# The first pair's expert layers as 64-row half products, and value sums and router additions on GpSimd

## The chip, the cores and the metric

The kernel runs on one core of a Trainium2 chip. The metric is the device time of one execution in microseconds (us). Five engines matter: TensorE (PE in the profile), VectorE (DVE), ScalarE (ACT), GpSimd (POOL) and the queue of SyncE (SP), which only issues DMAs here. Each engine takes its instructions in the order in which the program gives them.

## What is computed

There are 8 samples of 512 tokens and 256 features, each with 64 context rows and one conditioning row. In short:

```python
nx = layer_norm(x)                                  # (8, 512, 256)
weights = softmax(nx @ Wq @ (context @ Wk).T / 16)  # over 64 context rows
evidence = weights @ (context @ Wv)
combined = concat([nx, evidence, cond])             # 768 features
router_probs = softmax(combined @ router_W + router_b)          # 3 experts
h = silu(combined @ e_w1[e] + e_b1[e])              # 512 per expert
routed = sum over e of router_probs[e] * (h @ e_w2[e] + e_b2[e])
g = sigmoid(silu(combined @ gate_w1 + gate_b1) @ gate_w2 + gate_b2)
out = x + g * (routed @ out_w + out_b)
```

All of it is float32. A float32 product of 512 columns appears in the trace as two matmul instructions.

## The kernel before

Samples are worked in four pairs, j = 0 to 3. The two samples of a pair are the columns of a 2 x 2 block product, so that the nx part of each pair of hidden chunks takes seven products (called P1 to P7 here, `nx_operands`) in place of eight, over the sums T of the samples (`combine_x`) and ws of the weights (`combine_weights`, on GpSimd). The hidden layer has 14 chunks of 128: two of the gate (group 0) and twelve of the experts (groups 1 to 6). An expert layer e = 0, 1, 2 works two groups, `PAIRS[e]`, called a and b.

A group has three PSUM banks: U takes P1, P6, P7 and P4 in turn and is read after P1 (`keep_part` 0,0), after P6 (1,0), after P7 (`add` 1,1) and at the end (`silu` 0,1). Y takes P2 and is read by `add` 0,0. Z takes P5, is read by `keep_part` 1,1, then takes P3 and is read at the end. `keep_part` is a ScalarE copy to SBUF, `add` a VectorE addition to what is there, `silu` a ScalarE activation. The evidence part of every chunk is a product over only 64 context rows of each sample (`evidence`): sample 0 on rows 0 to 63 of the array and sample 1 on rows 64 to 127, the two side by side, in a stretch of its own between the layers.

In pairs 1 to 3 (`half_layers`) the nx products are also cut into a product over rows 0 to 63 and one over rows 64 to 127. A table of slots names two half products for each slot, which run side by side. The halves of one product lie two slots or more apart, and `half_product` makes TensorE wait for one half's end before the other half adds to the same bank. In pair 0 (`expert_layer`) the nx products are full, 128 rows. Between them stand, at points named S, A, B, C, D and E, the steps that `put(within, (e, point), ...)` places there: the second layer's weights e_w2 @ out_w (`second_layer`, eight products of 256 columns for each expert), the value products of pair 1 (`values_together`, products c1, c3, c5, c6 with sums of weights and values made by GpSimd and by accumulating DMAs), value weights of expert 2 (`value_weights`), the router of pair 0, the statistics and normalisation of pair 1's x, and the spread of the router's probabilities (`spread_probabilities`: four small DMAs to DRAM, then one that broadcasts them to all partitions, tile pb). `weigh` multiplies finished hidden chunks by them. `late_rows`, between layers 0 and 1, holds products with 32 columns of the array in bank 2, which VectorE reads.

The order in every engine's queue is the order of the program text (`tc.manual_schedule(engines=None)`). Waits between engines are placed by the framework.

## Time and profile before

| | us |
|---|---|
| median of 3 runs (lowest to highest) | 450.2 (450.2 to 450.43) |
| the profiled execution, its own time | 450.17 |
| its span, first to last instruction | 448.0 |
| TensorE busy | 443.1 (99%) |
| VectorE busy | 364.8 (81%) |
| ScalarE busy | 229.3 (51%) |
| GpSimd busy | 170.7 (38%) |

The profile shows one execution. Times on its axis begin at the span's start. The first pair's expert layers lie between 33.7 and 101.5 us, with the granted clock at 1.0 throughout. A busy TensorE is one with an instruction in flight; how close its instructions follow each other is read from their starts.

### The profile page before, as it was taken

How to read it: one execution, taken by the hardware profiler on the slowest of the kernel's cores; microseconds unless marked ns; L12 is line 12 of the kernel's file. 1: busy time of each engine (PE TensorE's matmuls, PEld its weight loads, DVE VectorE, ACT ScalarE, POOL GpSimd, SP SyncE). 2: the span in 40 equal slices, each digit the busy share in tenths (PEclk: the TensorE clock that was granted, in tenths of full speed). 3: DMA queues.
4: the chain of work that ended last, by engine and by line, in shares of the span. 5: the costliest groups of instructions: out<-in, count | busy, mean ns of one | idle time of the engine just before them, and what ended most of it. 6: DMA issues, size and time to landing. Idle time of an engine off the chain costs nothing.

```text
span 448.0 us, 5750 instructions
## 1 busy us (share of the span) xinstructions
PE 443.1 (99%) x1807; PEld 233.2 (52%) x1807; DVE 364.8 (81%) x686; ACT 229.3 (51%) x417; POOL 170.7 (38%) x219
## 2 busy tenths in 40 slices
PE   9999999999999999999999999999999999999996
PEld 8744646444444444444666444445666444445665
DVE  3888889677978999879886989879867846689875
ACT  3545685548424257678523187668251266766000
POOL 6566777530241157108738320000466500001360
PEclk9999999999999999999999999999999999999999
DMA  8987798655651579979974284710561392000715
GB/s 254 381 192 177 112 260 166 116 93 117 64 85 23 119 172 234 166 131 115 121 119 69 36 216 127 112 30 11 83 95 28 53 217 41 1 0 5 112 25 94
DMA packets 136182, 51.20 MB, mean 114 GB/s; under 512 B 107069, under 2 KB 129529, under 8 KB 135641
## 3 DMA queue, kind: packets, MB, share of 16 engines
q1 hardware_dynamic: 113776, 29.90, 32.0%
q0 software_dynamic: 15456, 19.90, 24.8%
q10 hardware_dynamic: 6921, 1.05, 1.4%
q8 instruction: 14, 0.23, 0.2%
q14 instruction: 15, 0.12, 0.1%
HBM read 31.23 MB, written 7.39 MB: 86 GB/s over the span
## 4 chain that ended last, share of the span: by engine, by line
PE 98%; DMA 1%; SPq 0%; DVE 0%; issue 0%; DVEq 0%
PE ps_u L1139 32%; PE ps_z L1139 13%; PE ps_y L1139 12%; PE ps_X L1139 7%; PE ps_Y L1139 7%; PE ps_V L1139 3%; PE ps_gu L1139 3%; PE ps_vc L1139 3%; PE ps_Z L1139 3%; PE ps_w2o L556 2%; PE ps_W L1139 2%; PE ps_vw L930 2%; PE ps_s L795 2%; PE ps_gz L1139 2%; DMA hall<-in_ctx_dram 1%; PE ps_tokens L1139 1%
## 5 line engine op out<-in xcount | busy, mean ns | idle before, releaser
L1139 PE MATMUL ps_u<-nxT,w 64*128 64x512 f32 (+1 forms) x184 | 86.8, 592 | 0.0
L1254 DVE TENSOR_TENSOR hall<-hall,pb 128x512 f32<-128x512 f32 x96 | 62.9, 694 | 12.2 <-ACT hall L1197 11.8
L1197 ACT ACTIVATE hall<-hall,abias 128x512 f32<-128x512 f32 x72 | 49.4, 718 | 25.0 <-DVE hall L1203 24.7
L1139 PEld LDWEIGHTS ps_u<-nxT,w 64*128 64x128 f32 (+1 forms) x184 | 33.1, 187 | 26.1 <-issue 21.8
L1139 PE MATMUL ps_z<-T,ws 64*128 64x512 f32 (+1 forms) x92 | 46.4, 590 | 0.0
L1139 PE MATMUL ps_z<-nxT,ws 64*128 64x512 f32 (+1 forms) x92 | 45.9, 590 | 0.0
L1139 PE MATMUL ps_y<-nxT,w 64*128 64x512 f32 (+1 forms) x92 | 45.5, 590 | 0.0
L1139 PE MATMUL ps_u<-T,ws 64*128 64x512 f32 (+1 forms) x92 | 42.8, 590 | 0.0
L1139 PE MATMUL ps_u<-T,w 64*128 64x512 f32 (+1 forms) x98 | 42.4, 589 | 0.0
L1206 ACT COPY hall<-ps_u 128x512 f32<-128x512 f32 x48 | 27.8, 579 | 13.2 <-PE ps_u L1139 12.5
L1634 POOL TENSOR_TENSOR hall<-hall 128x1026 f32<-128x1026 f32 x5 | 14.0, 2790 | 50.1 <-DVE hall L1631 50.1
L1139 PE MATMUL ps_z<-wT,vw 64*128 64x512 f32 x56 | 27.5, 596 | 0.0
L1631 DVE TENSOR_TENSOR hall<-hall 128x1026 f32<-128x1026 f32 x21 | 26.3, 1267 | 0.4
L1139 PEld LDWEIGHTS ps_z<-nxT,ws 64*128 64x128 f32 (+1 forms) x92 | 17.3, 188 | 13.3 <-issue 10.9
L1139 PE MATMUL ps_z<-wT,w 64*128 64x512 f32 x48 | 24.1, 589 | 0.0
L1139 PEld LDWEIGHTS ps_y<-nxT,w 64*128 64x128 f32 (+1 forms) x92 | 17.3, 188 | 13.0 <-issue 12.8
L1139 PEld LDWEIGHTS ps_z<-T,ws 64*128 64x128 f32 (+1 forms) x92 | 17.2, 188 | 12.8 <-issue 11.1
L1139 PEld LDWEIGHTS ps_u<-T,w 64*128 64x128 f32 (+1 forms) x98 | 16.2, 187 | 13.2 <-issue 12.1
L1139 PEld LDWEIGHTS ps_u<-T,ws 64*128 64x128 f32 (+1 forms) x92 | 16.1, 188 | 13.3 <-issue 11.7
L1203 DVE TENSOR_TENSOR hall<-hall,ps_z 128x512 f32<-128x512 f32 x24 | 16.3, 683 | 6.3 <-ACT hall L1206 3.0
L1197 ACT ACTIVATE hall<-ps_u,abias 128x512 f32<-128x512 f32 x24 | 16.4, 686 | 8.9 <-PE ps_u L1139 4.5
L594 POOL DMA_DIRECT2D other<-hall x1 | 1.3, 1332 | 50.1 <-ACT other L1664 50.1
(375 smaller groups left out, 1096.1 us busy)
## 6 DMA issues: line engine op xcount, KB each, us to landing
pb<-pd POOLq DMA_DIRECT2D x4, 1536.0 KB, 7.0
xb<-in_x_dram SPq DMA_DIRECT2D x64, 64.0 KB, 2.5
x<-in_x_dram SPq DMA_DIRECT2D x28, 128.0 KB, 3.6
hall<-hall POOLq DMA_DIRECT2D x6, 513.0 KB, 5.8
w<-in_L_xcond_e_w_dram SPq DMA_DIRECT2D x6, 512.0 KB, 11.0
xd<-x SPq DMA_DIRECT2D x24, 128.0 KB, 3.5
xg<-xd SPq DMA_DIRECT2D x48, 64.0 KB, 2.7
hall<-in_L_xcond_e_w_dram SPq DMA_DIRECT2D x3, 512.0 KB, 15.5
```

Of the source, the lines that this page charges most:

```text
L556: nc.tensor.matmul(ps[:, d * H : (d + 1) * H], w2T[:, k, (i + d) * P : (i + d + 1) * P], ow_sb[:, k, :], start=(k == 0 and d == 0), stop=T ...
L594: nc.gpsimd.dma_start(dst, src, accum_op=ALU.add)
L795: nc.tensor.matmul(ps[side(i, h), g * NH : (g + 1) * NH], mr[:, k, 2 * j + i, g * TB : (g + 1) * TB], S["nxT", 2 * j + i][:, k, h * NH : ( ...
L930: nc.tensor.matmul(ps, vT[:, k, j * 2 * CT : (j + 1) * 2 * CT], w1[:, KH + k, n0:n1], start=(k == 0), stop=(k == KH - 1),)
L1139: return nc.tensor.matmul(ps, lhsT, rhs, start=start, stop=True, skip_group_check=not start)
L1197: nc.scalar.activation(h, h if src is None else src, AF.Silu, bias=abias[:, c, 2 * j + i : 2 * j + i + 1])
L1203: nc.vector.tensor_tensor(h, h, part, ALU.add)
L1206: nc.scalar.copy(chunk(n, i, d), part)
L1254: nc.vector.tensor_tensor(h, h, S["pb", j][:, i, :, 2 * q // RC, :], ALU.mult)
L1631: engine.tensor_tensor(at[dst], at[p], at[m], ALU.subtract)
L1634: engine.tensor_tensor(at[dst], at[p], at[m], ALU.add)
```

## The change

`expert_layer` gives way to `first_pair_layer`, which works by a table of slots as pairs 1 to 3 do. A slot names the product of the first 64 rows and that of the last 64, and then the steps that follow: kID.n is `keep_part` of sample I and chunk D for group n, aID.n is `add`, sID.n is `silu`, @X runs what is put at point X, wN weighs N chunks, mGI copies finished second-layer weights. Second-layer products (20.0 to 22.3, two products of 256 columns each), the value products c1, c3.0, c3.1, c5, c6 and the value weights of expert 2 (v.0, v.1) are half products in these slots too; the last c3 product moves into the gate of the outputs.

```diff
-    def expert_layer(j, e, steps):
-        a, b = PAIRS[e]
...
+    FIRST_PAIR = (
+        (
+            "P1.b P5.a |",
+            "P2.a P1.a |",
+            "P4.g P1.b | k00.b",
+            "P1.a P2.a | k00.a a00.a",
+            "P2.b P4.g |",
+            "P5.a P6.b | k11.a @A",
+            "P6.a P5.b |",
+            "P6.b P2.b | k10.b",
+            "P3.a P6.a | k10.a gate s00.a",
+            "P7.b v.1 |",
+            "P5.b v.0 | k11.b",
+            "P7.a P7.b | a11.b early @C",
+            "v.1 P3.a |",
+            "v.0 P7.a | a11.a a00.b @B v s00.b s11.a s11.b rest",
+            "P3.b P4.b |",
+            "20.3 20.0 |",
+            "P4.b P4.a |",
+            "20.2 20.1 |",
+            "P4.a P3.b |",
+            "20.0 20.3 |",
+            "20.1 20.2 | m00 m02 @D",
+        ),
+        (
+            "P2.a P1.a |",
+            "c6 P1.b |",
+            "P1.a P5.a | k00.a",
+            "P1.b P2.a | k00.b odd a00.a",
+            "P5.a c6 | k11.a @c6 @N @A",
+            "c1.0 P6.a |",
...
+            "P7.a c5 | a11.a",
+            "P3.a P7.b | a11.b early w10 s11.a s11.b rest",
...
+        (
+            "P1.b P1.a |",
+            "P2.a P5.a |",
+            "P1.a P1.b | k00.a k00.b odd w2",
+            "P2.b P2.a | a00.a",
+            "P5.a P6.a | k11.a w2",
+            "P6.b P2.b | a00.b w1 @W @A",
+            "P6.a P5.b | k10.a s00.a",
+            "P3.a P6.b | k10.b",
+            "c3.0 P7.a |",
+            "P5.b P7.b | k11.b s00.b",
+            "P7.a c3.0 | @c3.0 a11.a",
+            "P7.b P3.a | a11.b early @C w6 s11.a s11.b rest",
+            "P3.b P4.a |",
+            "c3.1 P4.b |",
+            "P4.a P3.b |",
+            "P4.b c3.1 | @c3.1 @D",
+        ),
+    )
...
+        def half(token, k):
+            if token not in units:
+                units[token] = unit(token)
+            rows = row_half(k)
+            for ps, lhsT, rhs, part in units[token]:
...
+                yield half_product(ps, lhsT[rows, :], rhs[rows, :], k, fresh_, part)
...
+        for slot in FIRST_PAIR[e]:
+            products, after = slot.split("|")
+            both = [half(token, k) for k, token in enumerate(products.split())]
+            while both:
+                both = [one for one in both if next(one, both) is not both]
+            for token in after.split():
+                step(token)
```

`evidence` uses `half_product` as well. The router's additions go to GpSimd, the maximum between them stays on VectorE, and the value sums go from the start of layer 1 to layer 0's point B:

```diff
-        nc.vector.tensor_tensor(lg[:, 1:, :], le, lg[:, 1:, :], ALU.add)
+        if close and ED - 1 in es:
+            logit_sums(j, nc.vector)
...
+    def logit_sums(j, engine, biased=False):
+        lg, le = S["lg", j], S["le", j]
+        if not biased:
+            logit_bias(j, engine)
+        engine.tensor_tensor(lg[:, 1:, :], le, lg[:, 1:, :], ALU.add)
         mx = work.tile([P, NJ], F32, tag="rmx", name=f"rmx_{j}")
         nc.vector.tensor_reduce(mx, lg.rearrange("p e j -> p j e"), AX.X, ALU.max)
-        nc.vector.tensor_tensor(
+        engine.tensor_tensor(
             lg, lg, mx.unsqueeze(1).to_broadcast([P, E, NJ]), ALU.subtract
         )
...
+        elif at == (0, "C"):
+            home("yb", "na4", "na2", "a5", "a3")
...
+            add(V["a5"], v(1, 1), v(2, 1))
+            sub(V["na4"], v(2, 1), v(3, 1))
...
                 put(within, (0, "B"), combine_weights, 1)
                 put(within, (0, "B"), combine_weights, 2)
+                put(within, (0, "B"), logit_sums, 0, nc.gpsimd, True)
+                put(within, (0, "B"), values_together, 0, "C")
                 put(within, (0, "B"), combine_gate)
+                put(within, (0, "D"), combine_second, 0)
-                put(within, (0, "A"), router_logits, 0)
+                put(within, (0, "A"), router_logits, 0, range(ED), False)
+                put(within, (0, "A"), logit_bias, 0, nc.gpsimd)
...
-                put(within, (0, "C"), router_exp, 0)
-                put(within, (0, "D"), router, 0)
...
-                put(within, (0, "D"), spread_probabilities, 0)
...
+                put(within, (1, "S"), transpose_second, 1)
+                put(within, (1, "S"), router_exp, 0)
+                put(within, (1, "S"), anchor_columns, 1)
...
+                    for b, point in ((b0, "S"), (b1, "N")):
+                        put(within, (1, point), normalize, b)
+                        put(within, (1, point), store_x, b)
+                    put(within, (1, "N"), router, 0)
+                    put(within, (1, "N"), spread_probabilities, 0)
-                    put(within, (1, "B"), router_part, b0)
+                    put(within, (1, "A"), router_part, b0)
...
-                put(within, (2, "A"), gate_differences, 0)
+                put(within, (2, "A"), gate_differences, 0, (0, 1))
+                put(within, (2, "C"), gate_differences, 0, (2, 3))
```

## Rows read from the trace of the kernel before

**Rows 1.** The page, part 1: busy us (share of the span) xinstructions of each engine.
```profile
PE 443.1 (99%) x1807; PEld 233.2 (52%) x1807; DVE 364.8 (81%) x686; ACT 229.3 (51%) x417; POOL 170.7 (38%) x219
```
**Rows 2.** Waits of TensorE over the span: total us, times, longest.
```profile
PE ps_wake L332 <- PEq L2203: 0.8, 1, 0.8
PE pt_ctx L349 <- DMA hall<-in_ctx_dram: 0.3, 1, 0.3
```
**Rows 3.** Timeline of TensorE, evidence 0 and layer 0: start, us, operation, count.
```profile
29.17 1.02 PE L1139 MATMUL ps_u<-nxT,w 128*128 128x512 f32 x2
30.12 0.69 PE L1139 MATMUL ps_y<-wT,vw 64*128 64x512 f32 x1
...
33.23 0.59 PE L1139 MATMUL ps_z<-wT,vw 64*128 64x512 f32 x1
33.75 1.98 PE L1139 MATMUL ps_u<-nxT,w 128*128 128x512 f32 x4
35.57 1.02 PE L1139 MATMUL ps_u<-T,w 128*128 128x512 f32 x2
...
48.45 3.62 PE L556 MATMUL ps_w2o<-ow_sb,hall 128*128 128x256 f32 x16
...
53.23 0.69 PE L1139 MATMUL ps_u<-wT,vw 64*128 64x512 f32 x1
```
**Rows 4.** Timeline of TensorE, pair 1's layers, first and last step.
```profile
158.02 0.59 PE L1139 MATMUL ps_y<-nxT,w 64*128 64x512 f32 x1
...
205.66 0.59 PE L1139 MATMUL ps_z<-nxT,ws 64*128 64x512 f32 x1
```
**Rows 5.** Timeline of VectorE in layer 0.
```profile
33.01 0.69 DVE L1203 TENSOR_TENSOR hg<-hg,ps_w 128x512 f32<-128x512 f32 x1 [0.45 <-PE ps_w L1139]
33.61 0.69 DVE L786 TENSOR_TENSOR T<-nxT,T 128x512 f32<-128x512 f32 x1
...
45.73 1.29 DVE L548 STREAM_TRANSPOSE hall<-hall 128x512 f32<-128x512 f32 x2
```
**Rows 6.** Timeline of ScalarE in layers 0 and 1.
```profile
34.91 0.58 ACT L1206 COPY hall<-ps_u 128x512 f32<-128x512 f32 x1 [2.19 <-PE ps_u L1139]
...
36.63 0.69 ACT L1197 ACTIVATE hg<-ps_u,abias 128x512 f32<-128x512 f32 x1 [0.27 <-PE ps_u L1139]
37.22 1.32 ACT L1197 ACTIVATE hg<-hg,abias 128x512 f32<-128x512 f32 x2
...
56.46 1.28 ACT L695 ACT_TABLE_LOAD   x1
57.75 0.49 ACT L695 ACTIVATE sd<-mv,eps_t 128x4 f32<-128x4 f32 x2
```
**Rows 7.** Timeline of GpSimd in layer 0 and after it.
```profile
43.35 0.63 POOL L267 TENSOR_TENSOR ws<-w 128x256 f32<-128x256 f32 x1
...
48.30 0.64 POOL L270 TENSOR_TENSOR ws<-w,ws 128x256 f32<-128x256 f32 x1
...
50.65 2.10 POOL L910 DMA_DIRECT2D pd<-prT  x4
55.06 0.56 POOL L914 DMA_DIRECT2D pb<-pd  x1 [2.31 <-DMA pd<-prT]
```
**Rows 8.** Timeline of VectorE, layers 0 and 1.
```profile
48.62 0.75 DVE L686 BATCH_NORM_STATS2 st<-x 128x6 f32<-128x256 f32 x2
...
53.37 0.52 DVE L500 STREAM_TRANSPOSE ar<-ps_late 128x128 f32<-128x128 f32 x2 [0.65 <-PE ps_late L657]
...
58.30 3.68 DVE L705 TENSOR_SCALAR x<-x,mv,rstd 128x256 f32<-128x256 f32 x4
...
62.10 1.88 DVE L705 TENSOR_SCALAR x<-x,mv,rstd 128x256 f32<-128x256 f32 x4
...
72.89 3.09 DVE L1254 TENSOR_TENSOR hall<-hall,pb 128x512 f32<-128x512 f32 x5
```
**Rows 9.** The page, part 6, DMA issues: KB each, us from issue to landing.
```profile
pb<-pd POOLq DMA_DIRECT2D x4, 1536.0 KB, 7.0
```

More of the change, by code (lines that the diff above doesn't have):

```diff
@@ L548, in transpose_second, with second_unit, keep_second @@
             nc.vector.transpose(w2["T"][:, k, :], w2[e][:, k, :])
[L550 to L561 removed]
+    def second_unit(ps, i, d):
+        return [
+            (ps, w2["T"][:, k, (i + d) * P : (i + d + 1) * P], ow_sb[:, k, :], ps[:, d * H : (d + 1) * H])
+            for k in range(KH)
+        ]
+    def keep_second(e, i, ps):
+        c = e * RC + i
+        nc.scalar.copy(w2o[:, c : c + 2, :].rearrange("p c n -> p (c n)"), ps)
     def combine_second(e):
@@ L1139, in product, with half_product @@
         return nc.tensor.matmul(ps, lhsT, rhs, start=start, stop=True, skip_group_check=not start)
-    def half_product(ps, lhsT, rhs, half, start=False):
+    def half_product(ps, lhsT, rhs, half, start=False, out=None):
         prior_half, prior = last_half.get(ps.name, (half, None))
         if prior_half == half or start:
-            ins = product(ps, lhsT, rhs, start)
+            ins = product(ps if out is None else out, lhsT, rhs, start)
         else:
@@ L1158, in half_product @@
             nc.tensor.wait_ge(*finished[tag])
-            ins = product(ps, lhsT, rhs, start)
+            ins = product(ps if out is None else out, lhsT, rhs, start)
             tc.declare_fence(ins.ins, group=group)
@@ L1185, in evidence @@
             half = slice(i * CT, (i + 1) * CT)
-            product(ps, values(j, c)[half, c * P : (c + 1) * P], S["wT", j][half, :], start=start)
+            half_product(
+                ps, values(j, c)[half, c * P : (c + 1) * P], S["wT", j][half, :], i, start=start
+            )
     def chunk(n, i, d):
@@ L1319, in run, with first_pair_layer @@
+    VALUE_STEPS = {(1, c) for c in ("c6", "c1.0", "c1.1", "c5", "c1.2", "c1.3")} | {(2, "c3.0"), (2, "c3.1")}
+    W2O_BANKS = {(0, 0): 0, (0, 2): 4, (1, 0): 7, (1, 2): 4, (2, 0): 7, (2, 2): 6}
+    def first_pair_layer(e, steps):
+        j = 0
+        ns = dict(zip("ab", PAIRS[e]), g=0)
+        units, opened = {}, set()
         def run(point):
@@ new lines, in half @@
+        def half(token, k):
[3 more added lines that the diff above has]
+            for ps, lhsT, rhs, part in units[token]:
+                fresh_ = ps.name not in opened and (
+                    token[:2] in ("P1", "20", "21", "22") or token in ("v.0", "v.1")
+                    or isinstance(value_units.get(token, ("",))[-1], int)
+                )
+                opened.add(ps.name)
+                yield half_product(ps, lhsT[rows, :], rhs[rows, :], k, fresh_, part)
@@ new lines, in step @@
+        def step(token):
+            if token[0] == "@":
+                run(token[1:])
+                if (e, token[1:]) in VALUE_STEPS:
+                    values_together(e, token[1:])
+                    name = "c1" if token[1:3] == "c1" else "c3" if token[1:3] == "c3" else None
+                    if name:
+                        read_bank(V[name])
+                return
+            if token == "odd":
+                finish_odd(j, PAIRS[e - 1])
+            elif token == "gate":
+                finish_groups(j, (0,))
+                finish_odd(j, (0,))
+                silu(j, 0, 1, 1)
+            elif token == "v":
+                nc.scalar.copy(S["vw", j][:, 2 * RH : 3 * RH], units["vw"])
+                value_differences(j, 2)
+            elif token in ("early", "rest"):
+                for n in PAIRS[e]:
+                    (weigh_early if token == "early" else weigh_rest)(n)
+            elif token[0] == "w":
+                weigh(j, int(token[1:]))
+            elif token[0] == "m":
+                g, i = int(token[1]), int(token[2])
+                keep_second(g, i, units["w2o", g, i])
+            else:
+                kind, n = token.split(".")
+                n = ns[n]
+                i, d = int(kind[1]), int(kind[2])
+                if kind[0] == "k":
+                    part = Z[n] if d and i else U[n]
+                    keep_part(n, i, d, part)
+                    read_bank(part)
+                elif kind[0] == "a":
+                    part = Y[n] if not d else U[n]
+                    add(n, i, d, part)
+                    read_bank(part)
+                else:
+                    silu(j, n, i, d)
@@ L1875, in outputs @@
         nc.scalar.copy(g22, z)
+        run("first")
         spares(6, 7, 4)
@@ L2170 @@
             if j == 0:
-                for point in ("begin", "P1", "P6", "P2 half", "P2"):
+                for point in ("first", "begin", "P1", "P6", "P2 half", "P2"):
                     put(between, point, values_together, E, point)
@@ L2180 @@
                 for e in range(E):
[L2181 removed]
+                    first_pair_layer(e, within)
             outputs(j, between)
```

194 lines of the change are left out of this document (81 added, 113 removed).

## The prediction

> **What bounds the kernel now.** I read the engine totals first [rows 1]: TensorE is busy 443.1 of 448.0 us, VectorE 81%, ScalarE 51%, GpSimd 38%. Then the waits of TensorE [rows 2]: over the whole span it waits only twice, 0.8 and 0.3 us, both at the very start. Since a busy TensorE need not be a TensorE at its peak, I then checked the spacing of its starts. In layer 0 of the first pair the starts go from 35.57 to 48.45 us with 30 instructions between (15 full products of two instructions each): 12.88 / 30 = 0.4293 us each, 0.859 a product [rows 3]. Pair 1, which already works in half products, has 111 steps between 158.02 and 205.66: 0.4292 each, 0.858 a slot of two halves [rows 4]. So nothing waits in either form, and a slot of two halves costs what one full product costs. Splitting the products buys nothing by itself, and the pair's 67.8 us of layers can only shrink where the starts are not 0.429 apart.
>
> They are not where the product's shape changes. Around the first evidence (64-row products) the starts run from 29.17 to 35.57, 6.40 us, for 2 full instructions, 8 steps of halves and 4 full instructions [rows 3]. These 14 steps should take 6.01. The rest, 0.39, is two changes of shape: about 0.09 before the first instruction of the new shape and 0.10 in it. One change costs 0.195.
>
> **The change part by part.** *Fewer changes of shape.* The timeline of before has one change into and one out of halves at each of the four evidences, as in [rows 3]. With the layers in halves, five go: out of evidence 0, out of 1, in and out of 2, into 3. The late rows (32 columns) still separate layer 0 from evidence 1, so that pair of changes stays, and so does the one behind evidence 3. 5 x 0.195 = 0.98 us gained. Bounds: 0.78 if the change from halves to the late rows costs one more than from full products, and 0.98; no row shows more.
>
> *Second layer's and value products in halves*: 0. Counted in slots, layer 0 has 21 (14 products, the gate's last, two of value weights, four slots of second layer), layer 1 has 28, layer 2 has 16, as many products as before. The c3 product that leaves layer 2 for the gate is only moved.
>
> *New waits of TensorE.* A half's bank must be read before its next product, and the slots leave set distances. I lay slot n of layer 0 at 33.66 + 0.858 (n-1), 33.66 being 0.43 behind the evidence's last row at 33.23 [rows 3].
> (a) Slot 1 opens with P1.b in bank 1, which the gate's W product has just filled. VectorE reads W from 33.01 for 0.69 [rows 5], until 33.70. Before, this bank was opened a product later. Lost: 0.04 plus a signal, 0.08 (0 to 0.1).
> (b) In slot 9 ScalarE is given k10.a, three SiLUs of the gate and s00.a, and k11.b stands behind them. ScalarE starts 0.63 after a product's second instruction starts (34.91 [rows 6] against 35.57 - 3 x 0.429 = 34.28), and each operation overlaps the next by 0.10 (36.63 with 0.69, next at 37.22). Slot 9 starts at 40.53, so k10.a at 40.53 + 0.43 + 0.63 = 41.59. Then 0.48 + 0.59 + 1.22 + 0.62 puts k11.b at 44.50, done 45.08. VectorE's a11.b needs it: 45.12 to 45.81. P4.b's first half is in slot 15, 45.68, in the bank that a11.b reads: 0.15 late. Behind a11.b VectorE has two transposes, 1.29 [rows 5], and then a11.a: 45.12 + 0.60 + 1.29 = 47.01 to 47.70, for P4.a in slot 17, 47.39: 0.36 late with the signal. Both are on the second 64 rows, so they don't add: the later one counts. Lost 0.36 (bounds 0, if the queue runs a little faster than these rows, and 0.6).
> (c) Layer 1: the loads of the tables for Exp (moved to here) and Sqrt, 1.28 each [rows 6], stand ahead of k00.a. Evidence 1 starts at 53.5 (worked out below), so the SiLU of its second product ends at 53.5 + 0.1 + 0.86 + 1.06 + 0.6 = 56.1. Then come 1.28 + 0.25 for Exp, a copy 0.58, 1.28 + 0.49 for Sqrt [rows 6], and k00.a 0.58: 60.6. Slot 6 of layer 1 is at 53.5 + 0.1 + 4 x 0.858 + 5 x 0.858 = 61.3. Lost 0, with 0.7 spare.
> (d) Layer 2: k10.a follows slot 7 by 1.06, s00.a comes next, k10.b ends at 1.06 + 0.48 + 0.62 + 0.58 = 2.74, and P7.b in slot 10 is due 2.58 behind slot 7. Lost 0.2 (0 to 0.3).
>
> *Work given to GpSimd.* The three additions of the router leave VectorE (about 0.9 us), but the maximum between them stays, so VectorE now waits for GpSimd there. GpSimd comes to it behind the sums of two weights, 43.35 to 48.9 [rows 7], about 49.8. Behind it in VectorE's queue are value differences 0.7 and the statistics, which took 48.62 to 52.7 before (the transposes at 53.37 had waited 0.65) [rows 8], 4.1 us: 49.8 + 0.25 + 0.7 + 4.1 = 54.9, and with the transposes of the late rows (0.52 and a shorter one) 55.7. TensorE wants that bank in the fourth evidence slot. Evidence 1 began at 53.23 [rows 3]; now it begins 0.19 earlier for the lost change and 0.44 later for (a) and (b), 53.5, so the fourth slot is at 56.1. Lost 0, spare 0.4. The value sums go ahead of the layer 1 that uses them: 0.
>
> *Probabilities later.* They move from layer 0's end (first DMA at 50.65 [rows 7]) to slot 5 of layer 1, behind both normalisations. Four issues and the wait for their landing took 55.06 - 50.65 = 4.4, the broadcast lands 7.0 behind its issue [rows 7, 9]. VectorE stands in slot 18 before ten weighings of 0.62 [rows 8]; it is next needed by a00.a in layer 2, which waits for its product until about 88. Ten weighings, two additions and two weighings more are 8.7, so the landing may be as late as 79, and the first DMA as late as 67.8. Slot 5 is at 60.5 and the normalisations, 3.7 and 1.9 [rows 8], begin at about 60, so I place that DMA at 65.5 to 67. Lost 0; if this cover is gone, each us goes to TensorE.
>
> **Sum.** 0.98 - 0.08 - 0.36 - 0.2 = 0.34. The profiled execution took 450.17 us beside a span of 448.0, and the median of the runs is 450.2, the same within 0.03. 450.17 - 0.34 = 449.8. About 0.2%, 0.9 us, is what the measurement of this kernel can tell from no change.
>
> **The rivals.**
> (A) The waits of (a), (b) and (d) are all smaller than the gaps of the queues that I assumed. Speaking for it: they are each within 0.4 us of fitting. Then 450.17 - 0.98 = 449.2. Against: (b) is a plain sum of ScalarE rows. It must lose less than 0.1 in all to pass 0.2%.
> (B) Slower: VectorE stands at the router's maximum until GpSimd comes. The price is one us of TensorE for each us beyond the 0.4 spare, through the late rows' bank. The same normalisation takes 3.68 once and 1.88 the next time [rows 8], so work of these two engines side by side can double. Doubling one of the two weights' sums adds 2.8: 449.8 + 2.8 - 0.4 = 452.2. It decides from 1.7 us of delay on. Against: these same sums ran beside a busy VectorE before, and took 5.6.
> (C) Each half that hands its bank to the other half signals, 65 products, one signal each. In pair 1 the same hand-overs stand among 111 steps of 0.4292 [rows 4], where no price shows. The nearest price is the gap of 0.09 ahead of a change of shape; at a fourth of it, 0.02 a hand-over, 65 lose 1.4 us and the time is 451.2. I go by pair 1, 0. The Trainium skill, TensorE: Matmul & The Clock Gate, section The cost: per-tile semaphore tail, has increments serialise at 26.3 ns each; by that rule, if they lay on the path, the estimate is 65 x 0.026 = 1.7 us lost and 451.5, and pair 1 does not bear it out.
> (D) The change does not do what it says: the five changes go, but new waits eat them whole, as when (b) takes 0.6 and the late rows' bank 0.2 more. Then 450.2.
>
> **How the numbers follow.** The sum's own case (449.4 to 450.1) 0.50, A 0.20, D (450.1 to 451.0) 0.15, B 0.13, C 0.02. Faster by over 0.2% is A with little besides: 0.20. Within 0.2%: the sum's case and D, 0.65. Slower: B and C, 0.15. The predicted time is the sum, 449.8. The range from 449.2 (A, which no row allows to be passed) to 451.2 leaves out most of B and C.
>
> **What would show it.** Right: the half starts stay 0.43 apart from evidence 0 to the end of layer 0, with no 0.1 gap behind evidences 0, 1, 2 nor before 2 and 3. P1.b's first start is some 0.1 late. In layer 0 the products on the second 64 rows run 0.3 to 0.4 late from P4.a on, and in layer 2 0.2 late from P7.b. Evidence 3 ends about 0.3 us earlier than before. Wrong: VectorE idle at the router's maximum past 51 us, or at the first weighing past 79, or a gap of TensorE over 0.5 us anywhere in the pair's layers, or none at all.

## The result and the profile after

The changed kernel takes 452.7 us (median of 7 runs, 452.36 to 456.36), the kernel before 450.2 (7 runs beside them): 1.007 times as long, 95% interval 1.0043 to 1.0096. I had predicted 449.8, with 449.2 to 451.2 as the range. It is slower, by 2.5 us, and the prediction is wrong on both counts. The profiled execution took 452.36 us beside a span of 450.4; before, 450.17 beside 448.0.

The page of the changed kernel, part 1, against [rows 1], shows nothing of it: TensorE has more instructions for the halves, and the other engines are about as busy as before.

```profile
PE 443.4 (98%) x1961; PEld 242.9 (54%) x1961; DVE 362.6 (81%) x683; ACT 228.6 (51%) x416; POOL 171.2 (38%) x222
```

The waits of TensorE in the changed kernel (total us, times, longest) answer to [rows 2]. The second and the fourth are new.

```profile
PE ps_wake L332 <- PEq L2326: 0.8, 1, 0.8
PE ps_gu L1149 <- ACT racc L2002: 0.8, 1, 0.8
PE pt_ctx L349 <- DMA hall<-in_ctx_dram: 0.4, 1, 0.4
PE ps_vc3.0_1015 L1149 <- DVE hall L1215: 0.2, 1, 0.2
```

They are 1 us of the 2.4 by which the spans differ. To find the rest I took the start of each stage from TensorE's timelines and subtracted. The stages of every profile that matters are below, in us (the tail is from the start of the last group of token products to the end of the span). "Before, again" is a second profile of the unaltered kernel before, and "changed, again" one of the changed kernel. A stage that begins or ends with an evidence product is counted from that product's first start, on the first 64 rows. Two stages are not shown: they agree within 0.01, except that cutting products of the last pair's outputs (the last three rows) lengthens one of them from 41.37 to 41.55.

| | start | layer 0 | layer 1 | layer 2 | evidence 3 to pair 1 | pair 1's layers | outputs of 1, layers of 2 | tail | span |
|---|---|---|---|---|---|---|---|---|---|
| before | 30.12 | 23.11 | 27.90 | 17.57 | 58.36 | 49.12 | 97.92 | 4.62 | 448.0 |
| before, again | 30.04 | 23.11 | 28.06 | 17.57 | 58.36 | 49.12 | 97.92 | 4.74 | 448.2 |
| changed | 29.60 | 23.48 | 27.61 | 17.73 | 59.43 | 49.68 | 97.91 | 5.67 | 450.4 |
| changed, again | 29.67 | 23.48 | 27.61 | 17.52 | 59.74 | 49.70 | 97.91 | 5.98 | 450.9 |
| probabilities early | 29.91 | 23.47 | 27.61 | 17.17 | 58.55 | 49.13 | 99.15 | 6.32 | 450.6 |
| copy first | 29.95 | 23.48 | 27.61 | 17.17 | 58.56 | 49.12 | 99.06 | 5.66 | 449.9 |
| copy, tail | 30.36 | 23.48 | 27.61 | 17.67 | 58.50 | 49.12 | 98.54 | 4.75 | 449.5 |
| copy, tail, layer 0 | 30.20 | 23.04 | 27.61 | 17.57 | 58.58 | 49.13 | 99.07 | 4.83 | 449.5 |
| all | 29.96 | 23.04 | 27.61 | 17.17 | 58.55 | 49.13 | 98.14 | 4.73 | 447.8 |

From before to changed: -0.52 at the start (it varies between 29.6 and 30.7 over the profiles, with the wait for the first loads), +0.37, -0.29, +0.16, +1.07, +0.56, -0.01 and +1.05 in the tail. The sum is +2.4. The three layers that were changed are 0.24 longer together. Against the 0.52 won at the start stand 2.68 lost where the diff touches little or nothing: at the gate behind layer 2, in pair 1, and in the last 6 us.

**Layer 0.** TensorE's timeline of the changed kernel, around the end of evidence 0 and at slot 15 (start, us, count), answers to [rows 3].

```profile
32.71 0.59 PE L1149 MATMUL ps_z<-wT,vw 64*128 64x512 f32 x1
33.23 0.69 PE L1149 MATMUL ps_u<-nxT,w 64*128 64x512 f32 x1
...
45.06 0.59 PE L1149 MATMUL ps_u<-nxT,w 64*128 64x512 f32 x1
...
45.56 0.69 PE L1149 MATMUL ps_u<-T,w 64*128 64x512 f32 x1
```

P1.b starts 0.52 behind the row ahead of it instead of 0.43, and its first instruction is 0.10 longer (0.69): the shape does not change any more, and yet it costs the same 0.19, because it waits for VectorE's read of W. P4.b at 45.56 shows the same 0.10 behind its wait.

**The gate behind layer 2.** The timeline of TensorE there, and the instructions of SyncE's queue, GpSimd and ScalarE that lead to it, in order of time:

```profile
104.88 1.02 PE L1149 MATMUL ps_gz<-hg,gw2s 128*128 128x512 f32 x2
106.65 1.12 PE L1149 MATMUL ps_gu<-g_t,gw_sb 128*128 128x512 f32 x2 [0.76 <-ACT racc L2002]
```
```profile
67.60 8.56 SPq L530 DMA_DIRECT2D xg<-xd  x8
68.91 0.55 POOL L919 DMA_DIRECT2D pb<-pd  x1 [2.57 <-issue]
76.27 1.69 SPq L975 DMA_DIRECT2D v_G<-in_L_xcond_e_w_dram  x2
83.12 1.74 POOL L978 DMA_DIRECT2D v_G<-in_L_xcond_e_w_dram  x2 [8.03 <-issue]
92.38 2.25 POOL L978 DMA_DIRECT2D v_G<-in_L_xcond_e_w_dram  x1
100.30 0.53 SPq L1106 DMA_DIRECT2D v_G<-v_G  x1
100.93 0.56 SPq L1107 DMA_DIRECT2D w<-racc  x1
106.02 0.59 ACT L2002 COPY racc<-ps_gu 128x512 f32<-128x512 f32 x1 [2.07 <-DMA w<-racc]
```

And the kernel before, in the same views:

```profile
68.14 0.96 SPq L969 DMA_DIRECT2D v_G<-in_L_xcond_e_w_dram  x2
69.53 4.49 SPq L530 DMA_DIRECT2D xg<-xd  x8
73.87 2.40 POOL L972 DMA_DIRECT2D v_G<-in_L_xcond_e_w_dram  x2
90.44 1.21 POOL L972 DMA_DIRECT2D v_G<-in_L_xcond_e_w_dram  x1
98.80 0.54 SPq L1097 DMA_DIRECT2D v_G<-v_G  x1
99.43 0.56 SPq L1098 DMA_DIRECT2D w<-racc  x1
105.22 0.59 ACT L1879 COPY racc<-ps_gu 128x512 f32<-128x512 f32 x1 [0.73 <-PE ps_gu L1139]
```

The last of the accumulating DMAs into G3, KB and us from issue to landing, in the changed kernel and before:

```profile
v_G<-in_L_xcond_e_w_dram POOLq DMA_DIRECT2D x1, 256.0 KB, 7.9
...
v_G<-in_L_xcond_e_w_dram POOLq DMA_DIRECT2D x1, 256.0 KB, 4.7
```

Read them from the last row back. ScalarE's second copy of the gate overwrites tile t1, so it must wait until the DMA w<-racc has read it. That DMA stands in SyncE's queue behind the copy of G3 (v_G<-v_G), which waits for the last of GpSimd's accumulating DMAs into G3. In the changed kernel that one was issued at 92.38 instead of 90.44 and took 7.9 us instead of 4.7. So it landed at 100.25, and the copy of G3 went out at 100.30; before, it had landed at 95.18, long ahead of the copy at 98.80. GpSimd had stood idle for 8 us at an accumulation into tiles whose loads SyncE issued at 76.27 instead of 68.14, behind eight gathers of x that took 8.56 instead of 4.49, beside the late broadcast of the probabilities (68.91). The DMA that reads t1 is issued 1.5 us later, and TensorE loses 0.91 (1.77 from start to start for two instructions of 0.43).

**The tail.** TensorE's last products, and VectorE's sums behind them, are spaced as before. The queues of SyncE and ScalarE that issue the last output transfers, and the DMA queue q8 between 443.0 and 443.5 us (packets, MB, share of 16 engines), in the changed kernel:

```profile
439.92 7.13 SPq L2027 DMA_DIRECT2D out_dram<-hg  x8
441.78 2.86 ACTq L2027 DMA_DIRECT2D out_dram<-hg  x4
445.88 1.32 ACTq L1918 DMA_DIRECT2D out_dram<-y_rows  x3
```
```profile
q8 instruction: 1, 0.02, 11.6%
```

The same queues in the second profile of the kernel before:

```profile
438.65 5.79 SPq L1904 DMA_DIRECT2D out_dram<-hg  x8
...
442.79 2.60 ACTq L1796 DMA_DIRECT2D out_dram<-y_rows  x3
```

Eight issues take 7.13 instead of 5.79, and the last three start 3.1 us later, against 1.3 for TensorE. In the changed kernel q8, which brings a program in packets of 16 KB, moves one among these transfers; before, its last one came at 421 and none here. The page of the changed kernel counts 16 such packets, that of before 14. This was the theory (F) to test beside that of the late probabilities (T).

### The profile page after: what moved, and what is told of

The parts are those of the page before. It is cut to its first block, busy times and chain, and to the rows that moved or that the text cites. A ratio compares the mean times of both kernels' runs of the same rounds, so it can differ in the third digit from the quotient of the medians.

```text
span 450.4 us, 6065 instructions
## 1 busy us (share of the span) xinstructions
PE 443.4 (98%) x1961; PEld 242.9 (54%) x1961; DVE 362.6 (81%) x683; ACT 228.6 (51%) x416; POOL 171.2 (38%) x222
## 3 DMA queue, kind: packets, MB, share of 16 engines
q10 hardware_dynamic: 6921, 1.05, 1.4%
## 4 chain that ended last, share of the span: by engine, by line
PE 60%; DVE 1%; issue 0%; DVEq 0%
PE ps_u L1149 17%; PE ps_z L1149 7%; PE ps_X L1149 7%; PE ps_Y L1149 7%; PE ps_y L1149 7%; PE ps_V L1149 3%; PE ps_Z L1149 3%; PE ps_gu L1149 2%; PE ps_W L1149 2%; PE ps_gz L1149 1%; PE ps_tokens L1149 1%; DVE x L702 1%; PE ps_s L792 1%; PE ps_gy L1149 1%; PE ps_vw L935 0%
## 5 line engine op out<-in xcount | busy, mean ns | idle before, releaser
L1149 PE MATMUL ps_u<-nxT,w 64*128 64x512 f32 (+1 forms) x208 | 95.3, 592 | 0.0
L1149 PE MATMUL ps_z<-T,ws 64*128 64x512 f32 (+1 forms) x104 | 52.4, 590 | 0.0
L1149 PE MATMUL ps_z<-nxT,ws 64*128 64x512 f32 (+1 forms) x104 | 51.3, 589 | 0.0
L1149 PE MATMUL ps_y<-nxT,w 64*128 64x512 f32 (+1 forms) x104 | 50.4, 589 | 0.0
L1149 PEld LDWEIGHTS ps_u<-nxT,w 64*128 64x128 f32 (+1 forms) x208 | 36.4, 187 | 24.9 <-issue 18.6
L1149 PE MATMUL ps_u<-T,w 64*128 64x512 f32 x112 | 48.2, 591 | 0.0
L1149 PE MATMUL ps_u<-T,ws 64*128 64x512 f32 (+1 forms) x104 | 48.0, 590 | 0.0
L1149 PEld LDWEIGHTS ps_y<-nxT,w 64*128 64x128 f32 (+1 forms) x104 | 19.1, 187 | 12.7 <-issue 12.5
L1149 PEld LDWEIGHTS ps_z<-T,ws 64*128 64x128 f32 (+1 forms) x104 | 19.4, 187 | 11.5 <-issue 9.9
L1149 PEld LDWEIGHTS ps_u<-T,w 64*128 64x128 f32 x112 | 18.6, 187 | 9.7 <-issue 8.6
L1215 DVE TENSOR_TENSOR hall<-hall,ps_u 128x512 f32<-128x512 f32 x24 | 16.1, 682 | 4.0 <-ACT hall L1218 1.9
## 6 DMA issues: line engine op xcount, KB each, us to landing
w<-in_L_xcond_e_w_dram SPq DMA_DIRECT2D x6, 512.0 KB, 12.7
```

Of the source, the lines that this page charges most:

```text
L1149: return nc.tensor.matmul(ps, lhsT, rhs, start=start, stop=True, skip_group_check=not start)
L1215: nc.vector.tensor_tensor(h, h, part, ALU.add)
```

## The experiments

All are compared with runs of the kernel before on the same chip, whose medians were 450.36 to 450.64. The changed kernel has two medians, 452.7 and 453.5, because its runs scatter; differences to it are given against both.

**The changed kernel again**, as a control: 

> The changed kernel once more, unaltered, for a second profile. Theory T (a collision of transfers): the first pair loses against the kernel before because the probabilities' broadcast, now in layer 1, runs beside the regrouping of x, the loads of G2 and G3 come behind it, GpSimd stands 8 us before their sums, the value sum t1 is late, and ScalarE's copy of the gate's product into the row that t1 leaves waits 2.07 us for the DMA that reads it. T expects that wait here again, TensorE 1.3 us longer from the first evidence to the first step of pair 1 (128.25 against 126.94 us), while the 0.56 us in pair 1 and the 1.05 us behind the last product may go or stay. Rival C (chance of one execution): pair 0 within 0.3 us of the kernel before and the loss elsewhere.

453.5 us (4 runs, 452.81 to 454.0), ratio 1.0068 [1.0053, 1.0083]. The wait at the gate was 1.1, the tail 5.98: the same places.

**The loads of G2 and G3 ahead of the gathers of x**, in layer 1's slot 16:

```diff
-            "P7.b c1.1 | @C @c1.1",
+            "P7.b c1.1 | @c1.1 @C",
```

> The changed kernel with one exchange: the value step c1.1, which issues the loads of G2 and G3, comes ahead of point C, which issues the regrouping of x. T: GpSimd stands at most 3 us before the sums with G in place of 8.0, the DMA that reads t1 lands before the gate's second product is done, TensorE's wait of 0.9 us in the gate is gone and the time falls by about 0.9 us, to 451.8 if all else stays. The 0.47 us that c3.0 loses in layer 2 stay. Rival H (the half products themselves cost the time): no change, 452.7.

453.31 us, ratio 1.0063 [1.0046, 1.008]: no gain, and a miss. The gate's wait did go and GpSimd no longer stood still (its accumulations into G2 and G3 are issued at 73.39). But its sums now ran beside VectorE's weighings, which began at 78.14, when the broadcast landed, and of which the first five took 0.88 each in the mean instead of 0.62 [rows 8] (timeline of VectorE; below it the waits of TensorE):

```profile
78.14 4.38 DVE L1266 TENSOR_TENSOR hall<-hall,pb 128x512 f32<-128x512 f32 x5 [4.81 <-DMA pb<-pd]
```
```profile
PE ps_vc3.0_1015 L1149 <- DVE hall L1215: 1.2, 1, 1.2
```

TensorE lost 1.2 at c3.0 in layer 2, where a bank waited for VectorE. The wait had changed its place; since TensorE came to the gate that much later, this run doesn't show whether the order alone would have removed the wait there. It also lost 1.4 in pair 1's outputs and pair 2's layers (99.35).

**The probabilities early**: the router and its exponentials back in layer 0, the additions on VectorE, the four small DMAs ahead of GpSimd's value sums and the broadcast behind them; `combine_gate` goes to layer 1 for it. In part:

```diff
-                put(within, (0, "B"), logit_sums, 0, nc.gpsimd, True)
+                put(within, (0, "B"), router, 0)
+                put(within, (0, "B"), spread_probabilities, 0, 1)
...
-                put(within, (0, "B"), combine_gate)
+                put(within, (0, "B"), spread_probabilities, 0, 2)
...
-                    put(within, (1, "N"), router, 0)
-                    put(within, (1, "N"), spread_probabilities, 0)
+                    put(within, (1, "N"), combine_gate)
```

> The changed kernel with the router's probabilities back in layer 0: additions on VectorE, exponentials at point C, the four small DMAs ahead of the value sums and the broadcast behind them; the gate's weight sums go to layer 1 for it. The loads of G2 and G3 stay behind the regrouping. T: the broadcast lands before layer 1's slot 18, VectorE doesn't wait 3.7 us at the first weighing, the regrouping's eight issues take about 4.5 us in place of 8.6, GpSimd stands about 4 us less, the gate's wait is gone or under 0.2 us and c3.0's 0.47 us in layer 2 is gone: about 1.4 us less, 451.3. Rival O (only the order of the loads matters): the wait in the gate stays at 0.5 us or more. Rival H: no change.

451.16 us (9 runs), ratio 1.0023 [1.0009, 1.0036]: 1.5 to 2.3 less than the changed kernel. The losses in layer 2, at the gate and in pair 1 are all gone (see the table); the tail stays. The profiled execution was one of the longer ones, 452.35: it lost 1.24 in pair 1's outputs and pair 2's layers, at VectorE and ScalarE.

**Layer 0's order**: the gate's SiLUs and s00.a behind k11.b, and the banks of P1.a and P1.b exchanged in layer 0.

```diff
-            "P3.a P6.a | k10.a gate s00.a",
+            "P3.a P6.a | k10.a",
...
-            "P5.b v.0 | k11.b",
+            "P5.b v.0 | k11.b gate s00.a",
...
-                    U[m] = bank({"a": 3, "b": 1}[n], f"ps_u_{j}_{m}")
+                    U[m] = bank(({"a": 3, "b": 1} if e else {"a": 1, "b": 3})[n], f"ps_u_{j}_{m}")
```

> The changed kernel with two exchanges in layer 0: the gate's three SiLUs and s00.a come behind k11.b, and the groups a and b exchange their first banks there, so that P1.b doesn't open the bank that VectorE still reads. By the rows of the changed kernel the first costs 0.12 at P7.b and 0.25 at P4, the second 0.19. Expected: evidence 1 starts 22.9 us behind evidence 0 in place of 23.5, with no first instruction of 0.69 us inside the layer. T: the gate's wait for the transfer takes part of it back, so the time falls by 0 to 0.56 us. Rival H: halves cost what they cost, evidence 1 stays at 23.5.

455.15 us, ratio 1.0103 [1.0047, 1.016]: slower still. Yet layer 0 took 23.04 instead of 23.48, as expected of it. The time went at the gate again: 2.5 us of waiting for the same DMA. It was issued at 100.76, no later than in the changed kernel (100.93), but took 6.8 us instead of 5.0. Behind the wait the granted clock was at 0.50, the 1.2 GHz level, from 109 to 112.

**One part alone in the kernel before**: router_exp, router and spread_probabilities moved from layer 0 to the end of point (1, "S"), behind both normalisations.

```diff
-                put(within, (0, "C"), router_exp, 0)
-                put(within, (0, "D"), router, 0)
-                put(within, (0, "D"), spread_probabilities, 0)
...
                         put(within, (1, "S"), store_x, b)
+                    put(within, (1, "S"), router_exp, 0)
+                    put(within, (1, "S"), router, 0)
+                    put(within, (1, "S"), spread_probabilities, 0)
```

> The kernel before with one part of the change alone: the router's exponentials, probabilities and their spread moved from layer 0 (points C and D) to the start of layer 1, behind both normalisations. Theory T (the late broadcast holds up VectorE): the first weighing starts at about 75 to 77 us instead of 72.9 and the weighings run into GpSimd's sums and the transfers of the values; VectorE is late for layer 2 and TensorE loses 0.5 to 2 us before the second pair: 451 to 452. Rival (the late probabilities are harmless in themselves, and only cost in the half-product layers): 450.4 within 0.3.

454.76 us, ratio 1.0088 [1.0069, 1.0107]: 4.1 us slower, twice what was expected. The waits of TensorE in this run:

```profile
PE ps_u L1139 <- ACT hall L1206: 2.0, 1, 2.0
PE ps_vc L1139 <- DVE hall L1203: 0.9, 1, 0.9
```

The first weighing starts at 79.13, after 5.78 us of waiting for pb, and five take 5.23. The copy of ScalarE in the first row stands behind a SiLU that waits for VectorE too. The two waits are 2.9 of the 4.9 us by which layer 2 is longer (22.47). Behind them the granted clock fell to 0.50, the 1.2 GHz level, between 97 and 99 (us, busy us and count, granted clock, DMA share, GB/s):

```profile
95.00:100.00 5.00, 4.09 (x7) 0.66 0.19 34
```

So the move alone is harmful.

**The place of TensorE's program.** Products of 512 or 342 columns can be issued as two of half the columns, the same sums in nearly the same time, with more instructions:

```diff
+    cut = [24]
     def product(ps, lhsT, rhs, start=False):
+        if not start and cut[0] and lhsT.shape[0] == P and len(ps.shape) == len(rhs.shape) == 2 and ps.shape[1] == rhs.shape[1] > 300:
+            cut[0] -= 1
+            for s in (slice(0, rhs.shape[1] // 2), slice(rhs.shape[1] // 2, rhs.shape[1])):
+                ins = nc.tensor.matmul(ps[:, s], lhsT, rhs[:, s], start=False, stop=True, skip_group_check=True)
+            return ins
```

In the kernel before, 24 cuts in pair 0: 

> The kernel before, with 24 of its full products of 512 columns issued as two products of 256 columns each (layer 0 and 1 of the first pair): the same sums, 24 more matmuls in TensorE's program. Theory F (program code): the profile's q8 queue brings TensorE's program in pieces of 16 KB; before, the last piece lands at 421 us, in the changed kernel at 443, among the last output transfers, whose issues on ScalarE's queue come 1.0 to 1.7 us late. 24 more products should move before's last piece from 421 to about 441 to 442: the time from TensorE's last matmul group to the end of the span grows from 4.62 to 5.5 or more, and the time by 0.8 to 1.3, to 451.2 to 451.7. Rival (the tail of the changed kernel has to do with its own earlier transfers, or varies by chance): tail 4.6, time 450.4 within 0.3.

With 18 cuts: 

> The kernel before with 18 products cut instead of 24. With 24 the last piece landed at 438, just ahead of the output transfers of the last sums, and the tail stayed 4.6 us. Six products fewer are 24 instructions of TensorE, so the piece should land at 440.5 to 442.5, among these transfers. Theory F: SyncE's eight issues take 6.9 to 7.5 us instead of 5.8 and the tail grows to 5.4 to 6.3. Rival: tail 4.6, and the long issues of the changed kernel have another cause.

With 24 the packet came at 438.5, ahead of the eight issues, and the tail stayed 4.6: this test missed its place. With 18 it came just before 442, and the kernel before shows the long issues of the changed one (q8 between 441.5 and 442; the two queues):

```profile
q8 instruction: 1, 0.02, 10.9%
```
```profile
440.17 6.62 SPq L1911 DMA_DIRECT2D out_dram<-hg  x8
...
445.85 1.35 ACTq L1803 DMA_DIRECT2D out_dram<-y_rows  x3
```

Tail 5.3, a little under what was expected; time 452.0, ratio 1.0027 [1.0015, 1.004]. For the issues and the tail F holds in this direction. But the run with 24 cuts, whose tail is as before, also took 452.05 in the median (9 runs, 450.57 to 456.12): cutting products early costs about 1.4 us elsewhere. Its profile is of the fastest execution, 450.57, and shows 0.84 lost in pair 1's outputs and pair 2's layers and 0.21 in pair 1's layers; with 18 cuts 0.87 is lost in the former. The medians of these runs thus don't price the tail.

In the kernel with the probabilities early, 24 cuts; and the same with layer 0's order: 

> The changed kernel with the probabilities early (as in the run with that change alone, 451.16), and 24 products of pair 0's outputs and of the gate each issued as two of half the columns. Theory F: the last piece of program lands near 429 instead of 442.5, before the output transfers; the tail falls from 6.3 to 4.6 us, and the time from 451.16 to 450.0 to 450.4. Rival (chance): the same time as without, 451.2 within 0.4, tail between 5.0 and 6.3.

> As the kernel with the probabilities early and the code moved, and besides in layer 0 the gate's SiLUs and s00.a behind k11.b, with the banks of P1.a and P1.b exchanged. In the run that had this order alone, evidence 0 to evidence 1 took 23.04 us against 23.48 in the changed kernel, though the rest of that run lost more in the transfers ahead of the gate. With the probabilities early those transfers should not be late: 0.43 less than without this order, 449.6 to 450.0, and faster than the kernel before by 0.4 to 0.8. Rival (the order is itself what made that run slow): 1 us or more slower than the kernel without it.

The packet came at 434.8 and 435.4, the eight issues took 5.77 and 5.78, the tails 5.0 and 5.2 (6.3 without the cuts, 4.6 expected). But the medians are 451.58 and 451.48, no better than 451.16.

In the changed kernel, 24 cuts in pair 0, and then 24 cuts in the last pair's outputs only, which leaves all earlier pieces where they were:

```diff
-    cut = [24]
+    cut = [0]
...
+        if j + 1 == NP:
+            cut[0] = 24
         if j:
             twenty_products(j, run, gated, finish, store, last_gate)
```

> The changed kernel, with 24 full products of the first pair's gate and outputs each issued as two of half the columns, and nothing else. Theory F: the last piece of TensorE's program lands near 435 instead of 443, the eight issues of output transfers on SyncE's queue take 5.8 us again instead of 7.1, and the time from the last matmul group to the end falls from 5.7 to 4.6 or 5.0: 0.7 to 1.3 us less than the changed kernel (453.3), 452.0 to 452.6. Rival (the cut products cost as much as they give, as they did in the kernel before, where the profile shows no place for it): the same tail gain in the profile, but the median within 0.4 of 453.3.

> The changed kernel, with 24 products of the last pair's outputs (342 columns) each issued as two of 171, and nothing else: up to 405 us the program and the places of its pieces are those of the changed kernel, and only the last piece comes earlier. Theory F: it lands at 430 to 437 instead of 443, SyncE's eight issues take 5.8 us instead of 7.1 and the tail 4.6 to 5.0 instead of 5.7 to 6.0; 0.7 to 1.0 us less than the changed kernel, 452.4. Rival: the tail shortens, but the median stays at 453.3, because the rest of the changed kernel varies by as much.

Both tails shortened (4.9 and 4.8, issues 5.80 and 5.78), and neither median fell: 454.7 and 454.38 (6 runs each, up to 458). The profile of the second shows a place where the changed kernel scatters: its wait at the gate was 3.43 us. In five profiles of kernels that don't touch that queue's order the wait was 0.76, 1.06, 1.48, 2.46 and 3.43, and the DMA that reads t1, issued between 100.6 and 102.0, took 5.0 to 6.8 us; what decides that time is open. The rows below are TensorE's timeline there, and stretches of 5 us (busy us and count, granted clock, DMA share, GB/s).

```profile
104.79 1.02 PE L1156 MATMUL ps_gz<-hg,gw2s 128*128 128x512 f32 x2
109.24 2.07 PE L1156 MATMUL ps_gu<-g_t,gw_sb 128*128 128x512 f32 x2 [3.43 <-ACT racc L2009]
```
```profile
100.00:105.00 5.00, 5.00 (x14) 1.00 1.10 187
105.00:110.00 5.00, 1.57 (x3) 0.83 0.59 158
110.00:115.00 5.00, 5.00 (x9) 0.50 0.11 18
115.00:120.00 5.00, 5.00 (x13) 0.99 0.89 95
```

Behind the wait the granted clock is 0.50, the 1.2 GHz level, until 115, and products of 512 columns take 0.86 an instruction instead of 0.43: the three groups from 109.24 on take 5.30 us, where the kernel before takes 2.67.

**The copy of t1 ahead of the copy of G3**: two lines of the changed kernel exchanged.

```diff
+            nc.sync.dma_start(w(0, 0), V["t1"])
             nc.sync.dma_start(V["G5"], V["G3"])
-            nc.sync.dma_start(w(0, 0), V["t1"])
```

> The changed kernel with two adjacent transfers in SyncE's queue exchanged: the copy of t1, which the gate's second ScalarE copy waits for (0.8 and 1.1 us in the two profiles), ahead of the copy of G3, which waits for the last of GpSimd's accumulations. Theory T (the value transfers came late, and this copy is held behind one of them): it is issued near 99 instead of 100.9, the wait of TensorE at the gate goes, 0.8 to 1.1 us less, 452.2 to 452.6. Rival (it is the load on the transfer engines, not the place in the queue): the copy lands at 105 to 106 all the same, and the time stays 453.3 within 0.4.

451.77 us (5 runs, 451.19 to 452.45), ratio 1.0031 [1.0019, 1.0043]: 0.9 to 1.7 less than the changed kernel, from two lines. SyncE's queue and ScalarE's copy:

```profile
94.08 0.54 SPq L1106 DMA_DIRECT2D w<-racc  x1
98.77 0.47 SPq L1107 DMA_DIRECT2D v_G<-v_G  x1
```
```profile
104.93 0.59 ACT L2002 COPY racc<-ps_gu 128x512 f32<-128x512 f32 x1 [1.13 <-PE ps_gu L1149]
```

The copy of t1 is issued 6.9 us earlier and ScalarE waits for TensorE again. Pair 1's layers are back at 49.12 too.

**The kernel before, unaltered**, for a second profile: 

> The kernel before, unaltered, for a second profile. If the lengths of its stages are the kernel's own: the tail 4.6 us, SyncE's eight issues 5.8, 55.5 from the gate of the first pair to the second pair, 49.1 for the second pair's layers, each within 0.2. If they vary from execution to execution as those of the changed kernels do, some of them differ by 0.5 or more.

Every stage within 0.16 us, the tail within 0.12: the stages of this kernel are its own. Two profiles of the changed kernel differ by up to 0.31 (behind evidence 3, and in the tail), so single differences of that size between changed kernels prove little.

**The terms together**: copy first and 24 cuts in the last pair; with layer 0's order; with the probabilities early as well.

> The changed kernel with the copy of t1 ahead of the copy of G3, as before, and the last piece of program moved. If the two are separate terms they add: 451.8 less 0.7 to 1.0, 450.8 to 451.1. What is then left against the kernel before (450.4) should stand in the second pair's outputs, where the run with the copy alone waited for accumulating transfers of w2o and took 99.06 us to the third pair's gate against 97.92. Rival: no gain beside the copy, 451.8 within 0.3.

> As the one with copy and tail, and the gate's SiLUs behind k11.b in layer 0 with the banks of P1.a and P1.b exchanged: evidence 0 to evidence 1 falls from 23.48 to 23.04. Theory: the first pair then takes 126.4 us instead of 126.8, but the second pair's outputs give it back in their waits for transfers, so 450.6 to 451.1. If the gain stays: 450.4. Rival (the order itself costs, as it seemed when it ran alone): 452 or more.

> All of it: copy first, last piece moved, layer 0's order, and the router back on VectorE with the probabilities spread in layer 0. With the copy first, the early probabilities should have little left to give: within 0.3 of the kernel without them, 450.5 to 451.0. If they still gain 0.5 or more, the late probabilities cost through VectorE itself and not only through the copy.

| | median us (runs) | ratio to before |
|---|---|---|
| copy, tail | 451.25 (12) | 1.0015 [1.0006, 1.0025] |
| copy, tail, layer 0 | 450.77 (11) | 1.0011 [1.0003, 1.002] |
| all | 450.71 (12) | 1.0007 [0.9997, 1.0017] |

Against 451.77 with the copy alone the tail gives about 0.5 (in the profiles 0.91, less the 0.18 that the cuts cost in the last pair's outputs), layer 0's order 0.5 more (0.44 in the profile), the early probabilities 0.06, nothing. With intervals of 0.1% to each side, about 0.45 us, the first two of these are hardly told from nothing. With all of it the half products run as fast as the full ones, and not measurably faster. The profiled execution of this kernel took 449.59, but the median is 1.1 above it.

## Why the prediction was wrong

**The step that failed is "Probabilities later": "Lost 0; if this cover is gone, each us goes to TensorE".** I followed one consumer, VectorE's weighings, and placed the landing at up to 79. It landed at 76.7, inside that, and yet the move cost most of the 2.5 us. I had costed the broadcast as a wait of VectorE alone. What it also is: 1.5 MB beside the gathers of x, whose eight issues took 4.0 to 4.8 us in the profiles without the late broadcast and 5.4 to 12.7 in those with it. With SyncE's new order (gathers ahead of the loads of G2 and G3) this made GpSimd's value DMAs late, and one of them held, in SyncE's queue, an unrelated copy that the gate needs.

Two runs undo this at its two ends, the early probabilities (-1.5 to -2.3) and the copy first (-0.9 to -1.7), and either removes the loss at the gate and the 0.56 of pair 1. With the copy first the early probabilities gain 0.06: so in the changed kernel the late broadcast cost mainly through that queue. Through VectorE, as I had argued, it cost less: with the new order of the loads layer 2 took 17.17 to 17.73 in eight profiles with the broadcast late, and 17.17 in all four with it early. With the old order of the loads the same move does cost through VectorE, 1.2 at c3.0 in the changed kernel and most of 4.1 in the kernel before.

Part of my price was wrong too: I had ten weighings at 0.62, and in the changed kernel the eight of them that ran while GpSimd stood idle took that, the two beside its additions 1.19 each (VectorE):

```profile
76.76 3.10 DVE L1266 TENSOR_TENSOR hall<-hall,pb 128x512 f32<-128x512 f32 x5 [3.68 <-DMA pb<-pd]
...
84.23 2.38 DVE L1266 TENSOR_TENSOR hall<-hall,pb 128x512 f32<-128x512 f32 x2
```

**What I did not look at: the tail.** The sum has no term for it: +1.05 in the profile, about 0.5 in the median by one pair of runs (451.77 and 451.25). It comes from 154 more TensorE instructions of products, as many weight loads, and the hand-over waits, which shift the packets of the program. The Trainium skill, Runtime: NRT & Kernel Launch, section Instruction fetch mechanics, has the program come in blocks of 16 KB or 256 instructions, and the crossing mostly hidden. The traces agree on the 16 KB, and no wait of TensorE is put down to one; but the block is not hidden from the queues that issue output transfers: with one block among them SyncE's eight issues took 0.8 to 1.7 us longer, and the tail was 0.6 (kernel before with 18 cuts) to 1.3 us longer (probabilities early, against the same with 24 cuts).

**Fewer changes of shape**: 0.98 expected. Of the four changes in layers 1 and 2, 0.68 falls into these two stages (one's second half, 0.10, falls behind the start of evidence 3). Measured are 0.29 in layer 1 and 0.40 in layer 2 where no wait hides it, 0.69: this term was right. Of the fifth, in layer 0, 0.07 of 0.195 is left even with the order mended. Between evidence 3 and pair 1 0.13 to 0.30 is lost in the kernels with this change whose gate doesn't wait; most of that is (d).

**(a)** Expected 0.08, measured 0.19: behind the waits looked at here (0.02 to 0.76 us) the next instruction is longer by the same 0.1 as behind a change of shape, which I had not put in. **(b)** Right in kind: with the order changed, layer 0 gains 0.44 in all, for (a) and (b) together; I had 0.44. That the totals agree is partly luck, since 0.19 for (a) leaves 0.25 for (b) and not 0.36. **(c)** Right: no stall there. **(d)** Right where nothing hides it. In the profile of the changed kernel an earlier wait stands before it, 0.21 at c3.0 for VectorE (a00.b). With the probabilities early, ScalarE's k10.b ends at 92.31, and P7.b's second 64 rows start 0.21 behind the first rows of the slot; at evidence 3 they are 0.32 behind (TensorE, then ScalarE):

```profile
92.15 0.59 PE L1158 MATMUL ps_z<-T,ws 64*128 64x512 f32 x1
92.36 0.69 PE L1158 MATMUL ps_u<-nxT,w 64*128 64x512 f32 x1
...
98.16 0.59 PE L1158 MATMUL ps_u<-wT,vw 64*128 64x512 f32 x1
98.48 0.59 PE L1158 MATMUL ps_z<-wT,vw 64*128 64x512 f32 x1
```
```profile
91.74 0.57 ACT L1227 COPY hall<-ps_u 128x512 f32<-128x512 f32 x1
```

The table counts from the first 64 rows, so this turns up in the stage behind, where the gate's full products come only after both: 0.40 gained in layer 2 less 0.19 lost there is 0.21, and the sum had 0.49 - 0.2 = 0.29 for the two. The copy first shows the same.

**Work given to GpSimd**: VectorE stood at the router's maximum for 1.47 us until 49.35 (I had 49.8), and the late rows' bank cost TensorE nothing. Rival B is refuted.

**Rival C**: the 28 slots of layer 1 follow each other at 0.43 a step with all their hand-overs, so a signal shows no cost there, and the estimate by the Trainium skill's TensorE: Matmul & The Clock Gate, section The cost: per-tile semaphore tail, is not borne out here. **Rival D** was the nearest in kind: the gain is eaten whole. But it was eaten in other stages, and by more than the gain.

**What stays open.** The mended kernels lose 0.2 to 2.0 us in pair 1's outputs and pair 2's layers, at a wait for accumulating DMAs of w2o (up to 0.34) and at VectorE and ScalarE; the kernel before with 18 cuts waits there too (0.6). That a first pair that is done earlier gives its gain back there is not shown, and four runs speak against it: layer 0's order, the late probabilities in the kernel before, and the changed kernel with its two sets of cuts come to pair 1's outputs 1 to 5 us later than the changed kernel and lose 0.6 to 0.9 there as well. The 0.56 in pair 1 begins at a bank that waits for VectorE, which comes late out of the normalisation of x. Why that took 2.55 us for four instructions in the changed kernel, 2.11 with the copy first and 1.86 before, beside the same DMA issues of GpSimd, is open. It doesn't go with the gate's wait: pair 1's layers took 49.71 with the loads first, where the gate didn't wait, and 49.12 with cuts in the last pair only, where it waited 3.43. The cost of the early cuts is open too.

## What to carry to other kernels

When a step moves, follow its transfers past every queue, and not only its result to its first reader: ask what else each queue issues behind the transfer that now comes late, and look for a copy that could go ahead of it. A gain in one stage need not reach the end: with all terms together the first pair was 0.57 us shorter than before (126.37 against 126.94, from evidence 0 to pair 1), and the median was not. When instructions are added, see where the packets of the program land, above all among the last output transfers.

## What the runs showed of the hardware

A packet of 16 KB of TensorE's program among the output transfers lengthens eight DMA issues from 5.8 us (eleven profiles without one there) to between 6.6 and 7.5 (seven with one). The tails are 4.6 to 5.2 us without and 5.3 to 6.3 with one.

After pauses of TensorE of 0.8, 1.1 and 1.5 us the granted clock stayed at 1.00. After one of 2.5 us it fell to 0.50 for about 3 us, after one of 3.4 us for about 7 (its last us included), and after two of 2.0 and 0.9 us with one product between them for about 3. At 0.50 an instruction of 512 columns took 0.86 us instead of 0.43.

VectorE's weighing of 128x512 took 0.62 us while GpSimd stood idle and 1.19 beside its additions.
